# The third sum of each MLP weight set on GpSimd, from set 5 on

## The chip, the cores and the metric

The kernel runs on one core of a Trainium2 chip. The metric is the device time of one execution in microseconds (us). Each engine (TensorE or PE for matmuls, VectorE or DVE, ScalarE or ACT, GpSimd or POOL) works through its own queue in order, and so does SyncE (SP), which issues all DMAs of this kernel. Engines wait for each other through semaphores.

## The reference, cut to what matters

Two transformer blocks are applied to x, 32 sequences of 64 rows with 512 columns, all float32. The change touches only the MLP of the first block:

```python
def _L0_cond_ref(x, pos_ids, time_emb, ..., Wg, Wu, Wd):
    ...                                   # adaptive RMS norm, attention with rotary turning, x = res + ctx @ Wo.T
    res = x
    h = ada_rms(x, time_emb, ln2_w, ln2_tw)
    mlp = jax.nn.silu(h @ Wg.T) * (h @ Wu.T) @ Wd.T     # Wg, Wu: 2048 x 512, Wd: 512 x 2048
    return res + mlp
# second block: layer norm with scale and shift, latent keys and values, 16 heads of 32, x + out
```

## The kernel before, in words

The 2048 rows of x are worked in eight units of 256 rows. The MLP of a unit is cut into eight pieces (q modulo 8), each with 256 of the 2048 inner columns. A piece has three weight matrices of 2 x 2 blocks: gate (m = 0), up (m = 1) and down (m = 2). Each such product of 2 x 2 blocks is made with seven block products instead of eight, named P1 to P7, and for that each weight set needs four sums of its blocks.

A weight set is a tile `t` with seven slots of 128 x 256 float32. Slots 4 to 6 hold three blocks as they are loaded, the fourth block `a21` comes in a small tile of its own (two buffers), and slots 0 to 3 take the four sums. Slot 0 is `a21` + slot 6 (L288), slot 1 is slot 0 - slot 4 (L289), slot 2 is slot 4 - `a21` (L290), and slot 3 is slot 5 - slot 1 (L291). So the third sum (L290) needs only loaded data. The first and the third sum read `a21`, the fourth reads the second. `OF` (L254) says which product takes which slot: P1 slot 4, P6 slot 1, P5 slot 0, P7 slot 2, P2 slot 5, P3 slot 3, P4 slot 6.

The sets are numbered in the order of use: gate 0, up 0, gate 1, up 1, down 0, gate 2, up 2, down 1 and so on. The 24 sets of the first unit (numbers 0 to 22 and 25) are summed on the chip. Their four sums are written to DRAM (`done_with`, L296, "sums<-set"), and the other seven units load the finished sums from there (L274). So the sums are made once, while the MLP of the first unit runs, which in the profile is from about 60 to 155 us (sets 0 and 1 from 18 us on).

Five buffers hold the sets. When set n is done with, its sums are written out and set n + 5 is loaded (L269, and L272 for `a21`), both through SP's queue in order; a set's buffer is free when its products have been made and its write-out has read it. The load of an `a21` tile waits until the sums of the set two before it have read the old one. `combine(n + 2)` asks for the sums of a set two sets ahead of its use (L984 and L1045). Sets 0 and 1 are summed on GpSimd, the others on VectorE, but for the fourth sum, which is on GpSimd for all sets. Sets 2, 3 and 4 have their VectorE sums held behind a marked instruction (L281).

Around the sums, each piece q runs so: the first four products of gate and of up (`first_products`, L977, tile `gu` in PSUM), with ScalarE copying out P1 (L989, tile `e`) and VectorE adding P6, P5 and P7 to it (L991, L993, L996); then the first four products of the down matrix of the piece before (`down`, L1036); then the last three products of gate and up (`last_products`, VectorE's L1003), the gating (`gated`: VectorE's L1014 and GpSimd's L1015, then GpSimd's block sums L1017, L1018 and L1019 in tile `td`, which down reads), and the last three products of down. In a piece the last products of gate and up start only when L996 has read the `gu` bank.

Beside the first MLP the attention of the second unit ends, and VectorE works out the angles for units 2 and 3 (`angles(2)`, L368 to L397: many 128 x 128 operations). The order on the queues is made by the Tile framework's scheduler from the order of the program and its own model of times; the order by hand (`ordered`, `after`) holds only at the start and the end. So instructions of one engine can stand in another order than in the text.

Of the kernel before, what the change touches and what calls it, by code (L numbers as in the profile page):

```python
# [13 lines left out]
ALU = mybir.AluOpType  # L14
# [112 lines left out]
def two_blocks(ctx: ExitStack, tc: tile.TileContext, a: dict, out: bass.AP):  # L127
    nc = tc.nc
# [150 lines left out]
    def combine(n):  # L279

        with after(tc, mybir.EngineType.DVE, marks[0]) if 2 <= n < 5 else nullcontext():  # L281
            sums_of_set(n)

    def sums_of_set(n):
        if n < len(sequence) and sequence[n][1] < NP:
            t, a21 = sets[n], odd[n]
            e = nc.gpsimd if n < 2 else nc.vector
            e.tensor_tensor(t[:, 0], a21, t[:, 6], ALU.add)  # L288
            e.tensor_tensor(t[:, 1], t[:, 0], t[:, 4], ALU.subtract)  # L289
            e.tensor_tensor(t[:, 2], t[:, 4], a21, ALU.subtract)  # L290
            nc.gpsimd.tensor_tensor(t[:, 3], t[:, 5], t[:, 1], ALU.subtract)  # L291

    def done_with(m, q):
# [1006 lines left out]
```

## Time and profile before

| what | value |
|---|---|
| time of the kernel, median of 3 runs | 1027.22 us (1026.29 to 1027.46) |
| the profiled execution's own time | 1028.28 us |
| its span, first to last instruction | 1026.3 us |
| PE busy | 999.9 us (97%) |
| VectorE busy | 551.1 us (54%) |
| ScalarE busy | 327.3 us (32%) |
| GpSimd busy | 436.0 us (42%) |
| mean granted TensorE clock | 0.995 |

The execution that was profiled took 1028.28 us, 1.06 us more than the median of the runs; 1.98 us of it lie outside the span. TensorE is busy for nearly the whole span, so an operation on another engine matters only where TensorE waits for it.

### The profile page before, as it was taken

To read this page: it belongs to the slowest core of one execution; us is meant where nothing else is said; L and a number is where in the kernel's file an instruction comes from. 1 tells how busy PE (TensorE), PEld (TensorE's weight loads), DVE (VectorE), ACT (ScalarE), POOL (GpSimd) and SP (SyncE) were. 2 spreads that over 40 slices of the span, in tenths; PEclk is the share of its full clock that TensorE was granted. 3 is DMA by queue.
4 is the path that set the end of the run, shared out by engine and by line. 5 is a ranking of instruction groups with operands and counts; after the bars stand their busy time and mean duration, and the time that the engine had idled before them with its cause. 6 is when DMAs were issued, how large, how long until landed. Compare 5 with 4: busy or idle time off the path is not lost.

```text
span 1026.3 us, 21720 instructions
## 1 busy us (share of the span) xinstructions
PE 999.9 (97%) x8726; PEld 931.3 (91%) x8726; DVE 551.1 (54%) x1376; ACT 327.3 (32%) x652; POOL 436.0 (42%) x519
## 2 busy tenths in 40 slices
PE   8999899999999989999999999999999999999998
PEld 7789899988999989989989999899999899999986
DVE  5767866535355485344663366552565425554374
ACT  4432113245214242142340342242323512334032
POOL 4335546344154442346342354333553343644252
PEclk9999999999999998999999999999999999999999
DMA  9636898273555564555436755464735538751201
GB/s 349 243 120 233 274 373 302 83 252 109 194 207 181 192 242 149 200 211 204 143 117 218 258 172 191 166 230 175 288 104 195 237 119 331 290 215 38 93 1 42
DMA packets 68850, 198.54 MB, mean 193 GB/s; under 512 B 7312, under 2 KB 16272, under 8 KB 68368
## 3 DMA queue, kind: packets, MB, share of 16 engines
q1 hardware_dynamic: 68752, 197.17, 53.0%
q8 instruction: 69, 1.13, 0.4%
q14 instruction: 29, 0.24, 0.1%
HBM read 180.37 MB, written 16.78 MB: 192 GB/s over the span
## 4 chain that ended last, share of the span: by engine, by line
PE 84%; DVE 7%; DMA 3%; POOL 3%; ACT 2%; issue 1%; SPq 0%; POOLq 0%; DVEq 0%; ACTq 0%
PE gu L977 34%; PE down L1036 17%; PE q L565 11%; PE po L565 10%; DMA set<-in_wmlp 2%; PE pp L600 2%; PE sc L909 1%; PE lat L565 1%; PE kv L565 1%; PE cx L939 1%; PE sc L723 1%; PE cx L744 1%; DVE sm L593 1%; DMA stays<-in_wqkv 1%; PE tab L436 1%
## 5 line engine op out<-in xcount | busy, mean ns | idle before, releaser
L977 PE MATMUL gu<-h,set 128*128 128x128 f32 x2048 | 289.0, 278 | 7.0 <-DVE c L996 2.1
L977 PEld LDWEIGHTS gu<-h,set 128*128 128x128 f32 x2048 | 260.0, 193 | 16.3 <-issue 9.9
L977 PE MATMUL gu<-hc,set 128*128 128x128 f32 x1536 | 216.0, 277 | 0.0
L977 PEld LDWEIGHTS gu<-hc,set 128*128 128x128 f32 x1536 | 194.0, 193 | 1.6 <-issue 1.1
L1015 POOL TENSOR_TENSOR act<-c,c 128x384 f32<-128x384 f32 x64 | 66.8, 1043 | 195.8 <-DVE c L1003 158.1
L1036 PE MATMUL down<-td,set 128*128 128x128 f32 x1024 | 138.1, 277 | 2.9 <-POOL td L1018 2.1
L1036 PEld LDWEIGHTS down<-td,set 128*128 128x128 f32 x1024 | 125.5, 192 | 5.9 <-POOL td L1018 2.9
L989 ACT COPY e<-gu 128x128 f32<-128x128 f32 x128 | 33.9, 264 | 268.7 <-PE gu L977 261.8
L1003 DVE TENSOR_TENSOR c<-gu,u 128x256 f32<-128x256 f32 x128 | 53.4, 419 | 109.6 <-PE gu L977 109.1
L1036 PE MATMUL down<-act,set 128*128 128x128 f32 x768 | 109.8, 278 | 0.0
L565 PE MATMUL po<-cT,stays 128*128 128x256 f32 x480 | 108.4, 380 | 0.8 <-ACT cT L754 0.7
L565 PE MATMUL q<-h,stays 128*128 128x256 f32 x480 | 109.0, 381 | 0.0
L1036 PEld LDWEIGHTS down<-act,set 128*128 128x128 f32 x768 | 98.0, 192 | 6.0 <-issue 3.7
L991 DVE TENSOR_TENSOR u<-e,gu 128x128 f32<-128x128 f32 x128 | 36.0, 282 | 125.0 <-ACT e L989 121.3
L565 PEld LDWEIGHTS po<-cT,stays 128*128 128x128 f32 x480 | 89.3, 190 | 12.2 <-ACT cT L754 1.1
L565 PEld LDWEIGHTS q<-h,stays 128*128 128x128 f32 x480 | 89.6, 190 | 11.6 <-ACT r_a L464 0.3
L595 POOL TENSOR_TENSOR p<-p,sm 128x512 f32<-128x512 f32 x40 | 41.3, 1051 | 131.1 <-DVE sm L594 117.5
L576 POOL TENSOR_TENSOR qT<-u_q,v_q 128x512 f32<-128x512 f32 x30 | 38.1, 1271 | 88.2 <-DVE v_q L575 88.2
L621 DVE TENSOR_TENSOR x<-x,po 128x512 f32<-128x512 f32 x28 | 19.2, 685 | 72.2 <-PE po L565 70.0
L1072 ACT ACT_TABLE_LOAD x35 | 44.9, 1283 | 26.5 <-DVE c L1003 26.0
L1072 ACT ACTIVATE c<-gu 128x128 f32<-128x128 f32 x64 | 17.7, 277 | 105.2 <-DVE c L1003 104.5
L1017 POOL TENSOR_TENSOR td<-act 128x256 f32<-128x256 f32 x64 | 47.0, 734 | 5.6 <-DVE act L1014 0.9
(264 smaller groups left out, 1320.3 us busy)
## 6 DMA issues: line engine op xcount, KB each, us to landing
set<-sums SPq DMA_DIRECT2D x168, 512.0 KB, 6.6
set<-in_wmlp SPq DMA_DIRECT2D x192, 384.0 KB, 5.6
sums<-set SPq DMA_DIRECT2D x24, 512.0 KB, 4.0
x<-in_x SPq DMA_DIRECT2D x8, 512.0 KB, 5.7
mod<-in_mod SPq DMA_DIRECT2D x7, 512.0 KB, 7.9
a<-in_wmlp SPq DMA_DIRECT2D x24, 128.0 KB, 5.4
out_x<-x SPq DMA_DIRECT2D x12, 256.0 KB, 2.4
stays<-in_wo SPq DMA_DIRECT2D x2, 1024.0 KB, 9.6
```

The lines of the kernel that those rows point to most:

```text
L565: nc.tensor.matmul(ps, w[:, k, cols], h[:, k, :], start=(k == 0), stop=(k == KC - 1))
L576: nc.gpsimd.tensor_tensor(dst, u, v, ALU.add)
L595: nc.gpsimd.tensor_tensor(p8, p8, sm.unsqueeze(2).to_broadcast(wide), ALU.mult)
L600: nc.tensor.transpose(pp[:, c, :], p[:, c * P : (c + 1) * P], ident)
L977: nc.tensor.matmul(ps, w[:, slot, k * P : (k + 1) * P], b[of][:, k], start=start and k == 0, stop=k == 1, skip_group_check=True)
L989: nc.scalar.copy(e, ps[:, 0])
L991: nc.vector.tensor_tensor(u2, e, ps[:, 1], ALU.add)
L1003: nc.vector.tensor_tensor(c.rearrange("p (a b) t -> p a b t", b=2)[:, :, 1], ps[:, 2:4], u2.unsqueeze(1).to_broadcast([P, 2, HT]), ALU.add,)
L1015: nc.gpsimd.tensor_tensor(act[:, 1:4], gate[:, 1:4], c[:, 1:4], ALU.mult)
L1017: nc.gpsimd.tensor_tensor(td[:, 0:2], act[:, 1:3], act[:, 0:2], ALU.subtract)
L1036: nc.tensor.matmul(sums_of[u][p][:, c], w[:, slot, c * P : (c + 1) * P], b[of], start=q % NP == 0 and i % 2 == 0 and c == 0, stop=q % NP = ...
L1072: nc.scalar.activation(gate[2][:, 0], gate[0][:, 0], AF.Silu)
```

## The change

The third sum (slot 2) of each set from number 5 on goes to GpSimd, where VectorE made it. For sets 0 and 1 it was on GpSimd before, and for sets 2 to 4 it stays on VectorE. That makes 19 of the 24 sums of this kind (sets 5 to 22 and 25). In the kernel after the change the third sum stands at L291 and the fourth at L292; all lines from there on have a number higher by one.

```diff
             e = nc.gpsimd if n < 2 else nc.vector
             e.tensor_tensor(t[:, 0], a21, t[:, 6], ALU.add)
             e.tensor_tensor(t[:, 1], t[:, 0], t[:, 4], ALU.subtract)
-            e.tensor_tensor(t[:, 2], t[:, 4], a21, ALU.subtract)
+
+            (e if n < 5 else nc.gpsimd).tensor_tensor(t[:, 2], t[:, 4], a21, ALU.subtract)
             nc.gpsimd.tensor_tensor(t[:, 3], t[:, 5], t[:, 1], ALU.subtract)
```

## The prediction

> **What bounds the kernel now.** I read the page first, then the busy time by stage around the first MLP, the waits of TensorE there, the rows of the sums, and the order of time on VectorE and GpSimd.
>
> ```profile
> PE 999.9 (97%) x8726; PEld 931.3 (91%) x8726; DVE 551.1 (54%) x1376; ACT 327.3 (32%) x652; POOL 436.0 (42%) x519
> ```
>
> TensorE is busy for 97% of the span, so all engines together keep it waiting for 26.4 us. The change can only win where one of these waits ends on VectorE beside the first MLP. The stages there (us; then busy us and instructions of PE, weight loads, VectorE, ScalarE, GpSimd; granted clock, DMA share, GB/s):
>
> ```profile
> 60.00:98.00 38.00, 37.37 (x326) 36.07 (x327) 28.04 (x66) 10.87 (x22) 18.04 (x23) 1.00 0.64 219
> 98.00:118.00 20.00, 16.15 (x136) 15.30 (x135) 19.24 (x69) 2.57 (x9) 8.49 (x10) 1.00 0.71 236
> 118.00:152.00 34.00, 33.94 (x305) 33.77 (x303) 21.62 (x59) 4.44 (x15) 17.55 (x25) 1.00 1.01 354
> ```
>
> Only from 98 to 118 us is TensorE short of work: 20.00 - 16.15 = 3.85 us, with VectorE busy for 19.24 of 20 us (the angles are in its queue). Before it lie 0.63 us, after it 0.06 us. In the middle stage TensorE waits for (us in all, times, longest):
>
> ```profile
> PE gu L977 <- DVE ang L393: 1.5, 1, 1.5
> PE gu L977 <- DVE prod L383: 1.4, 1, 1.4
> PE gu L977 <- DVE c L996: 0.8, 2, 0.6
> PE down L1036 <- DVE set L289: 0.2, 1, 0.2
> ```
>
> All are VectorE's. The first two are named by whatever VectorE finished last; at 103.69 and 115.89 us TensorE starts last products of gate and up, which need L996, and L996 started at 103.27 and 115.47 us. So VectorE's queue ahead of L996 sets TensorE's time here. The moved sum and the ones beside it (durations: least, median, most, in ns):
>
> ```profile
> L290 DVE TENSOR_TENSOR set<-set,a x22: 410/418/1224, 62.0 to 147.7; 128x256 f32<-128x256 f32 x22
> L290 POOL TENSOR_TENSOR set<-set,a x2: 724/725/726, 18.8 to 24.2; 128x256 f32<-128x256 f32 x2
> ```
>
> The same sum takes 418 ns on VectorE and 725 ns on GpSimd. How the two engines hinder each other is seen in the order of time; these rows are from one moment (start, duration):
>
> ```profile
> 109.64 0.42 DVE L288 TENSOR_TENSOR set<-a,set 128x256 f32<-128x256 f32 x1 [0.61 <-DMA set<-in_wmlp]
> ...
> 110.45 0.28 DVE L379 TENSOR_TENSOR prod<-prod,stays 128x128 f32<-128x128 f32 x1
> 110.65 0.42 DVE L290 TENSOR_TENSOR set<-set,a 128x256 f32<-128x256 f32 x1
> 110.99 0.82 DVE L389 TENSOR_TENSOR stays<-stays,prod 128x128 f32<-128x128 f32 x1
> ```
>
> ```profile
> 110.67 0.99 POOL L291 TENSOR_TENSOR set<-set 128x256 f32<-128x256 f32 x1 [1.73 <-DVE set L289]
> ```
>
> L379 and L389 have the same kind and size; alone it takes 0.28 us, beside GpSimd's fourth sum 0.82 us, and that sum takes 0.99 us against its shortest 0.72. They exclude each other. Last, what SP's write-out of the sums waited for in the middle stage:
>
> ```profile
> SPq L296 <- DVE set L290: 7.3, 4, 2.4
> SPq L296 <- POOL set L291: 2.2, 3, 0.9
> ```
>
> **The change part by part.** The sum is made against the profiled execution: 1028.28 us, which is its span of 1026.3 and 1.98 around it. It lies 1.06 us above the median of the runs, so a difference found here is applied to the median, 1027.22 us.
>
> *Removed from VectorE:* 19 sums. The 22 rows of L290 add to 13.61 us; the three that stay (sets 2 to 4: 0.42, 0.95, 0.41) leave 11.83 us. One row starts 0.34 us after the one before it where nothing hinders it (110.65 to 110.99). Six lie in the middle stage; the last (117.14) is behind the last wait of TensorE. Five count: 5 x 0.34 = 1.7 us taken out of the queue ahead of L996. The other 13 lie where TensorE is busy throughout, but for sets 5 and 6 below: worth nothing; their cover is TensorE's own work (37.37 of 38 and 33.94 of 34 us).
>
> *Added to GpSimd:* 19 x 0.725 = 13.8 us, so its busy time goes from 436.0 to about 450 us. In the middle stage it has 20 - 8.49 = 11.5 us free, for 6 x 0.725 = 4.4. In the last stage a piece of the MLP takes 9.4 us (first down products at 122.22, 131.60 and 141.28 us); GpSimd is idle between its fourth sums there for 0.41, 0.95 and 0.95 us (from 121.34 to 126 us), which is where three sums of 0.73 fit. Queued behind a new sum are L291 of the same set, which needs L289 anyway, and at the next piece L1015 to L1019. Those have room: at 120.74 us L1018 has ended, and the product that reads it starts at 122.66. Cover gone, each sum would cost up to 0.73 us per set.
>
> *Blocking of VectorE by the new sums.* In the middle stage, ten VectorE rows of the angles are longer than the shortest of their kind and size (for the cast L368, 0.75 us, 0.28 is taken): 0.47, 0.33, 0.11, 0.65, 0.53, 0.22, 0.22, 0.54, 0.33 and 0.17, together 3.57 us, beside 8.49 us of GpSimd work. That is 0.42 us per us of GpSimd, so a sum of 0.725 us gives back 0.30 us, and five give back 1.5 us. Bounds: nothing, where VectorE is then at PSUM work or finds the gap (L991, with one input in PSUM, keeps its 0.28 us beside GpSimd), and 0.725 each, 3.6 us, where each blocks in full. I take 1.5, as it comes from the same stage and the same operations.
>
> The Trainium skill (SBUF — State Buffer, section "Who interferes with whom") says that a VectorE instruction with two SBUF inputs contends with a GpSimd instruction that reads SBUF, and that the first to issue holds the port for its whole length. The rows above agree. By that rule alone, with VectorE always at such work, each moved sum would cost 0.725 and save 0.34 us: a loss of 0.39 us each, 1.9 us for five. It is the rule that speaks against this change.
>
> *SP's queue.* No DMA is added or moved, but the write-out L296 and the next load of `a21` (L272) now wait for GpSimd's third sum. In the middle stage L296 waited 7.3 us for VectorE's L290, which stood behind angles (set 12: L288 at 104.07, L290 only at 106.88 us). On GpSimd the third sum can go as soon as the data is there. What that is worth: set 13's load was issued at 103.32 us, behind the write-out at 102.89, and VectorE sat idle 0.61 us until it landed. The write-out can't go before set 11's fourth sum (101.54 to 102.86), which comes earlier by the two L290 ahead of it, less the blocking. Bounds 0 and 0.61 us of idle time; I take 0.4 gained, nearer the upper one, since L296 is freed of its larger wait.
>
> *Sets 5 and 6.* At 78.52 us TensorE had waited 0.59 us for L621 of VectorE (77.78), which stood behind L290 rows of 0.67 and 0.96 us. Bounds: 0.59 us gained, and 0.3 lost if the new sums beside L288 and L289 block longer than what goes. I take 0.3 gained; it passes on, since set 10's load (90.69 us) waits for TensorE.
>
> Sum: -1.7 + 1.5 - 0.4 - 0.3 = -0.9 us. 1028.28 becomes 1027.4; the median 1027.22 becomes **1026.3 us**. What is late next in the middle stage is VectorE still: it keeps some 19 of 20 us. By the skill's rule in place of the measured share, the sum would be +1.9 - 0.4 - 0.3 = +1.2 us.
>
> **The rivals.** (A) *VectorE relieved in earnest.* Little blocking, as the sums fall beside PSUM work or in VectorE's idle time, and loads land earlier: the removed 1.7 us, the 0.61 and the 0.59 are won, 2.9 us, 1024.3 us. At the very most all 3.85 + 0.59 = 4.4 us of waits go: 1022.8. For it: 7.3 us of SP waits for L290. Against: the stretched rows.
>
> (B) *Slower: the new sum heads GpSimd's queue and waits for its load.* If it stands ahead of L1015, L1017 and L1018 wait for the DMA. VectorE's L288 shows when data is there: 95.98, 109.64, 120.00 and 129.85 us for the first sets of four pieces. Add 0.73 for the sum and the time from L1015's start to L1018's end (2.80, 2.53, 2.63, 2.33): `td` is ready at 99.5, 112.9, 123.4 and 132.9 us. The reading product started at 98.75, 110.68, 122.66 and 132.04. Losses 0.8 + 2.2 + 0.7 + 0.9 = 4.6; less the 0.9 gained above, +3.7 us: 1030.9. It decides once data lands over about 1.2 us after L1015 could start (in the piece at 118.11: 122.66 - 2.63 - 0.73 = 119.3). For it: the sum stands earlier in the program than L1015 and has no other input. Against: in all four pieces VectorE's L288 stands behind L1014, which starts with L1015, so the order now holds the load to come later.
>
> (C) *The order doesn't follow.* The scheduler may put VectorE's angles ahead of L996 in the freed places. Then TensorE's waits stay, and the time is that of before, 1027.2 us, with up to 1 us either way.
>
> **How the numbers follow.** My forecast, a wash to a small gain, 0.34; C 0.10; A 0.27; B 0.26; something else 0.03. A measurement of this kernel can tell about 0.2%, 2.05 us, from no change. Forecast and C lie within it for nearly all of their chance, with the forecast's ends from the bounds: -1.7 + 0 - 0.61 - 0.59 = -2.9 and -1.7 + 3.6 + 0 + 0.3 = +2.2. So: faster 0.30 (A, and the forecast's lower end), within 0.40, slower 0.30 (B, the full blocking, and part of the rest). The range takes in A and most of B: 1023.3 to 1030.6 us. The likeliest case alone: 1024.3 to 1029.4.
>
> **What would show it.** In the changed kernel the third sum is L291 and the fourth L292: 21 on GpSimd near 0.73 us and 3 on VectorE. VectorE's busy time falls by less than 11.8 us (blocking on L288, L289 and the angles). From 98 to 118 us TensorE's busy time stays at 16 to 18 us and VectorE's above 18. Waits of SP for a VectorE third sum are gone. After 160 us nothing changes. Wrong: TensorE busy there over 18.5 us (A); waits of L1036 for `td`, and GpSimd idle until a set's load in front of L1015 (B); TensorE's waits after 160 us, or the granted clock, differing by over 1 us (an order upset elsewhere).

## The result, and the profile after

The changed kernel takes 1032.65 us (median of 7 runs, 1028.43 to 1034.44); the kernel before took 1027.22 us (7 runs). The ratio is 1.0054 with a 95% interval of 1.0042 to 1.0066: the change costs about 5.4 us, and the forecast of 1026.3 us and its whole range (to 1030.6) are missed on the slow side.

The execution whose profile follows took 1034.44 us (span 1032.6 us), 1.8 us above its median. Busy time and instructions of the engines in it, from its page:

```profile
PE 999.9 (97%) x8726; PEld 930.3 (90%) x8726; DVE 550.0 (53%) x1357; ACT 327.6 (32%) x652; POOL 449.1 (43%) x538
```

The 19 instructions have moved, and GpSimd has 13.1 of the 13.8 us that were worked out for it (436.0 to 449.1). But VectorE has lost only 1.1 us of busy time (551.1 to 550.0), where instructions of 11.8 us were taken away. TensorE does the same work as before (999.9 us), in a span 6.3 us longer. The same stages beside the first MLP as in the prediction (us; then busy us and instructions of PE, weight loads, VectorE, ScalarE, GpSimd; granted clock, DMA share, GB/s):

```profile
60.00:98.00 38.00, 37.71 (x330) 36.52 (x331) 25.74 (x60) 11.12 (x22) 20.20 (x26) 1.00 0.65 221
98.00:118.00 20.00, 13.73 (x113) 12.70 (x111) 19.73 (x57) 1.49 (x5) 12.14 (x18) 1.00 0.58 196
118.00:152.00 34.00, 30.75 (x264) 29.96 (x265) 19.54 (x49) 4.72 (x16) 20.43 (x28) 1.00 0.91 308
```

TensorE is idle in the first for 0.29 us (before 0.63), in the middle one for 6.27 us (before 3.85) and in the last for 3.25 us (before 0.06). That is 5.6 us more from 98 to 152 us, about the whole loss, and a good half of it lies in the stage whose sums had been put down as covered. What TensorE waited for from 60 to 160 us (the five largest; us in all, times, longest):

```profile
PE gu L978 <- DVE c L997: 3.5, 6, 1.1
PE gu L978 <- DVE stays L379: 2.8, 2, 1.5
PE down L1037 <- POOL td L1019: 1.8, 1, 1.8
PE gu L978 <- DVE h L562: 0.8, 1, 0.8
PE down L1037 <- DVE set L289: 0.8, 1, 0.8
```

The wait for VectorE's L997 (L996 before) has grown from 0.8 to 3.5 us, and there is a new wait of 1.8 us for GpSimd's `td`, the sign that the prediction had announced for rival B. The moved sums themselves are as priced: 21 on GpSimd of 729 ns, 3 on VectorE.

```profile
L291 POOL TENSOR_TENSOR set<-set,a x21: 719/729/966, 20.1 to 155.7; 128x256 f32<-128x256 f32 x21
L291 DVE TENSOR_TENSOR set<-set,a x3: 413/418/947, 62.2 to 65.7; 128x256 f32<-128x256 f32 x3
```

**Where the new wait comes from.** GpSimd in the order of time (start, duration; in brackets the idle time before it and what ended it):

```profile
92.09 0.73 POOL L496 TENSOR_TENSOR tot_a<-sq_a 128x256 f32<-128x256 f32 x1
96.67 0.94 POOL L291 TENSOR_TENSOR set<-set,a 128x256 f32<-128x256 f32 x1 [3.86 <-DMA set<-in_wmlp]
97.58 1.17 POOL L1016 TENSOR_TENSOR act<-c,c 128x384 f32<-128x384 f32 x1
98.83 0.79 POOL L1018 TENSOR_TENSOR td<-act 128x256 f32<-128x256 f32 x1
99.69 0.52 POOL L1019 TENSOR_TENSOR td<-act,td 128x128 f32<-128x128 f32 x1
```

and the product that reads `td`:

```profile
100.26 1.60 PE L1037 MATMUL down<-td,set 128*128 128x128 f32 x12 [1.80 <-POOL td L1019]
```

The third sum of set 10 heads GpSimd's queue, and GpSimd stands idle for 3.86 us until that set's load lands. The gating (L1016), which started at 93.92 us before, starts at 97.58 us behind it, the block sums follow, and TensorE waits 1.80 us.

**Where VectorE's time went.** Its rows beside GpSimd's L1016 and L1018:

```profile
97.82 1.21 DVE L786 TENSOR_TENSOR hc<-h,hc 128x256 f32<-128x256 f32 x1
98.96 0.94 DVE L289 TENSOR_TENSOR set<-set 128x256 f32<-128x256 f32 x1
```

The same two took 0.67 and 0.41 us before. L289 makes slot 1 of set 10, which the product at 100.26 us reads too; it ended at 97.93 us before and at 99.90 us now, only 0.3 us ahead of `td`. From 60 to 160 us the means of L288 and L289 rose from 496 and 515 ns to 580 and 665 ns.

**What happened in the last stage.** SP's write-outs waited longer. From 60 to 160 us, first in the kernel before (for GpSimd and for VectorE's third sum, 69.8 us together), then in the changed one:

```profile
SPq L296 <- POOL set L291: 62.0, 15, 29.3
SPq L296 <- DVE set L290: 7.8, 5, 2.4
```

```profile
SPq L297 <- POOL set L292: 83.4, 18, 28.1
```

And they stand elsewhere. In the kernel before, SP issued the load of set 19 (L269) between the write-outs of sets 16 and 17 (L296):

```profile
122.51 0.33 SPq L296 DMA_DIRECT2D sums<-set  x1
122.89 0.42 SPq L272 DMA_DIRECT2D a<-in_wmlp  x1
123.40 1.69 SPq L269 DMA_DIRECT2D set<-in_wmlp  x2
125.20 0.38 SPq L296 DMA_DIRECT2D sums<-set  x1
```

In the changed kernel both write-outs (L297) come first, and then the loads of sets 19 to 21:

```profile
126.42 0.33 SPq L297 DMA_DIRECT2D sums<-set  x1
126.80 1.16 SPq L272 DMA_DIRECT2D a<-in_wmlp  x1
128.15 0.33 SPq L297 DMA_DIRECT2D sums<-set  x1
128.57 1.70 SPq L269 DMA_DIRECT2D set<-in_wmlp  x3
```

The write-out at 128.15 us follows at once on the end of GpSimd's fourth sum of set 17:

```profile
126.36 0.91 POOL L291 TENSOR_TENSOR set<-set,a 128x256 f32<-128x256 f32 x1
127.22 0.91 POOL L292 TENSOR_TENSOR set<-set 128x256 f32<-128x256 f32 x1
```

Counted from the first down product of set 16 (122.22 us before, 125.12 after), the load of set 19 is issued 3.45 us later where it was 1.18. VectorE's first sum of that set starts 10.30 us after the same product, where it was 7.63 (at 129.85 us):

```profile
135.42 0.42 DVE L288 TENSOR_TENSOR set<-a,set 128x256 f32<-128x256 f32 x1 [4.12 <-issue]
```

No DMA had been edited. The scheduler, which orders every queue by its own model of times, had moved the write-outs of sets 12, 17 and 20 in front of the loads of sets 14 and 15, of 19 and 20, and of 22.

### The profile page after: what moved, and what is told of

Same layout as the page of the kernel before. It is cut to its first block, busy times and chain, and to the rows that moved or that the text cites. A ratio compares the mean times of both kernels' runs of the same rounds, so it can differ in the third digit from the quotient of the medians.

```text
span 1032.6 us, 21704 instructions
## 1 busy us (share of the span) xinstructions
PE 999.9 (97%) x8726; PEld 930.3 (90%) x8726; DVE 550.0 (53%) x1357; ACT 327.6 (32%) x652; POOL 449.1 (43%) x538
## 3 DMA queue, kind: packets, MB, share of 16 engines
q8 instruction: 70, 1.15, 0.4%
## 4 chain that ended last, share of the span: by engine, by line
PE 84%; DVE 7%; POOL 3%; DMA 2%; issue 1%; ACT 1%; SPq 0%; POOLq 0%; DVEq 0%; ACTq 0%
PE gu L978 34%; PE down L1037 17%; PE q L566 11%; PE po L566 10%; PE pp L601 2%; PE sc L910 1%; PE lat L566 1%; PE kv L566 1%; PE cx L940 1%; DMA set<-in_wmlp 1%; PE sc L724 1%; PE cx L745 1%; DVE sm L594 1%; PE tab L437 1%; DMA mod<-in_mod 1%
## 5 line engine op out<-in xcount | busy, mean ns | idle before, releaser
L1016 POOL TENSOR_TENSOR act<-c,c 128x384 f32<-128x384 f32 x64 | 66.7, 1042 | 197.7 <-DVE c L1004 154.8
L566 PEld LDWEIGHTS q<-h,stays 128*128 128x128 f32 x480 | 89.5, 190 | 11.8 <-ACT r_a L465 0.3
L1018 POOL TENSOR_TENSOR td<-act 128x256 f32<-128x256 f32 x64 | 47.1, 736 | 5.4 <-DVE act L1015 0.6
```

The lines of the kernel that those rows point to most:

```text
L566: nc.tensor.matmul(ps, w[:, k, cols], h[:, k, :], start=(k == 0), stop=(k == KC - 1))
L1016: nc.gpsimd.tensor_tensor(act[:, 1:4], gate[:, 1:4], c[:, 1:4], ALU.mult)
L1018: nc.gpsimd.tensor_tensor(td[:, 0:2], act[:, 1:3], act[:, 0:2], ALU.subtract)
```

## The experiments

Three theories were set against each other. **Queue (Q):** the sum of set 10 at the head of GpSimd's queue makes `td` late. **SP's order (S):** loads are issued behind write-outs that wait for GpSimd. **Blocking (X):** GpSimd's sums hold up VectorE by more than is taken from it. Ratios are to the kernel before on the same chip in the same session (medians 1026.50, 1026.82 and 1027.01 us), with 95% intervals. A table of all kernels' stages stands at the end.

In the recorded expectations X is called P; O stands for a new order on VectorE and SP, and L for write-outs and loads that are late because GpSimd's fourth sums are.

The mean clock granted in an execution differs (0.991 to 1.000), and the time follows it. So some differences are also given *at equal clock*: one straight line of time against clock through the 204 executions of all kernels whose clock is on record, with a level of its own for each kernel and session, has a slope of 0.83 us per 0.001 of clock, and the levels are compared (with 95% limits). This is an estimate from those runs.

### The two halves of the change apart

*The relief alone.* From set 5 on, ScalarE copies a block into slot 2 and no engine makes the third sum; the subtraction is left out.

```diff
-            (e if n < 5 else nc.gpsimd).tensor_tensor(t[:, 2], t[:, 4], a21, ALU.subtract)
+            if n < 5:
+                e.tensor_tensor(t[:, 2], t[:, 4], a21, ALU.subtract)
+            else:
+                nc.scalar.copy(t[:, 2], t[:, 4])
```

> From set 5 on the third sum is left out and ScalarE copies its first operand (slot 4) to slot 2 instead: the subtraction is missing, so the numbers are not the reference's. VectorE is relieved as in the changed kernel and has its order (but for two neighbours swapped), SP has exactly its order; GpSimd's work and order are those of the kernel before. Theory P or Q (the loss is GpSimd's): the loss goes, 1027.2 us or less, down to 1024.3 if VectorE's relief is won in full. Theory O (order of VectorE and SP): 1030 us or more.

Measured: 1025.37 us, 0.9984 [0.9975, 0.9993], 1.1 us below the kernel before by the medians, 1.6 by the ratio and 0.8 +- 0.7 at equal clock. VectorE is busy for 544.0 us, 7.1 less.

*The load alone.* The kernel before, in which GpSimd makes each third sum from set 5 on once more into a tile that nobody reads. The order on the other four queues is that of before.

```diff
             e.tensor_tensor(t[:, 2], t[:, 4], a21, ALU.subtract)
+            if n >= 5:
+                junk = work("junk", [P, 2 * P], f"junk_{n}", 1)
+                nc.gpsimd.tensor_tensor(junk, t[:, 4], a21, ALU.subtract)
```

> The kernel before with 19 sums more: from set 5 on GpSimd makes the third sum once more into a tile that nobody reads, and VectorE keeps its own. PE, VectorE, ScalarE and SP have exactly the order of the kernel before; GpSimd has nearly that of the changed kernel, the extra sum of set 10 ahead of L1016 too. Theory P or Q (GpSimd's added work alone does it): as slow as the changed kernel or slower, 1032 us or more, as VectorE isn't relieved here. Theory O: 1029.5 us or less.

Measured: 1032.5 us, 1.0058 [1.0043, 1.0072], 6.0 us slower, with 1.01 us of waiting for `td` and 0.40 us for VectorE's third sum (L291 in this kernel). Engines' busy time, first the relief alone, then the load alone:

```profile
PE 996.9 (97%) x8726; PEld 928.6 (91%) x8726; DVE 544.0 (53%) x1357; ACT 334.3 (33%) x671; POOL 434.5 (42%) x519
```

```profile
PE 1001.1 (97%) x8726; PEld 931.7 (90%) x8726; DVE 558.6 (54%) x1376; ACT 327.2 (32%) x652; POOL 450.8 (44%) x538
```

VectorE's work in the second is that of before, yet it is busy for 7.5 us more: 0.39 us for each of the 19 sums. The changed kernel against the first gives (550.0 - 544.0) / 19 = 0.32 us. The other kernels with 19 moved sums give less: 0.28 with SP's order held, 0.22 with set 10's sum held, and 0.21 with both (549.3, 548.2 and 547.9 us). The prediction had 0.30, for the middle stage. So blocking is there, over the whole kernel at about the forecast's size; for the middle stage by itself no run gives it. And not all that VectorE gets back comes from the new sums: with none of them it has lost 7.1 us where rows of 11.8 us were taken away. The load costs several times what the relief brings, and nearly all of it in the middle stage (29.09 us from set 10 to set 16 against 23.91); the last stage runs at TensorE's full pace (28.14 us).

### The queue

*The sum of set 10 behind `td`.* The third sum of set 10 is held until GpSimd has issued the last block sum of `td` of that piece; the order on the other queues stays.

```diff
-            (e if n < 5 else nc.gpsimd).tensor_tensor(t[:, 2], t[:, 4], a21, ALU.subtract)
+            with after(tc, mybir.EngineType.Pool, ends_td[2]) if n == 10 else nullcontext():
+                (e if n < 5 else nc.gpsimd).tensor_tensor(t[:, 2], t[:, 4], a21, ALU.subtract)
...
+        ends_td[q] = latest(tc, mybir.EngineType.Pool)      # end of td, in gated
```

> The changed kernel with one difference: on GpSimd the third sum of set 10 is held behind the block sums of td of the piece before (L1020 of piece 2); all other instructions stand in the same order on all engines. Theory Q (the loss is GpSimd's queue waiting for set 10's load, 3.86 us in front of L1016, for which TensorE then waits 1.80 us): the wait of TensorE for td at 100.3 us goes, and the time falls from 1032.65 by 1.8 us or more, to 1030.9 or, if the later waits are its consequence, to about 1028. Theory P (the shared port: GpSimd's added work holds VectorE up): the time stays within 1 us of 1032.65. Theory O (the new order on VectorE and SP): it stays within 1 us too.

Measured: 1029.84 us, 1.0039 [1.0024, 1.0055]. The wait for `td` is gone; 0.60 us of waiting for VectorE's L289 stands at its place:

```profile
99.42 1.57 PE L1039 MATMUL down<-td,set 128*128 128x128 f32 x12 [0.60 <-DVE set L289]
```

*The sum of set 10 left on VectorE.*

```diff
-            (e if n < 5 else nc.gpsimd).tensor_tensor(t[:, 2], t[:, 4], a21, ALU.subtract)
+            (nc.gpsimd if n < 2 or (n >= 5 and n != 10) else e).tensor_tensor(t[:, 2], t[:, 4], a21, ALU.subtract)
```

> The changed kernel with the third sum of set 10 alone back on VectorE (18 moved sums are left). Theory Q: GpSimd no longer waits for that load in front of L1016, TensorE's 1.80 us wait for td goes: 1030.9 us or less. Theory P: one sum of 19 less on GpSimd, a gain of 0.3 us at most. Theory O: depends on the order that results; the order on VectorE after the angles is another one here, so a change either way of up to 2 us.

Measured: 1027.86 us, 1.0018 [1.0004, 1.0032]. Here 1.38 us of waiting for L289 stand in place of the 1.80 us for `td`. One of 19 sums left where it was takes away two thirds of the loss, but not by that wait alone: set 10's load landed only at 98.1 us in the profiled execution, and the load of set 19, too, is issued 2.82 us after the first down product of set 16, where the changed kernel has 3.45.

### Which sets cost

Only sets 5 to 9, only 10 to 15, or all from 16 on go to GpSimd:

```diff
-            (e if n < 5 else nc.gpsimd).tensor_tensor(t[:, 2], t[:, 4], a21, ALU.subtract)
+            (nc.gpsimd if 5 <= n < 10 else e).tensor_tensor(t[:, 2], t[:, 4], a21, ALU.subtract)
```

In the others the bounds are 10 and 16, and 16 and 26; `e` stays GpSimd for sets 0 and 1 and VectorE for the rest.

> Only the third sums of sets 5 to 9 on GpSimd, the others on VectorE; PE and SP have the order of the kernel before. The prediction's step on sets 5 and 6: a gain of up to 0.59 us (TensorE's wait for L621 at 78.5 us goes), about 1026.2 us, if nothing is blocked; a port effect here would show as a loss of at most 0.5 us, as TensorE is busy from 79 to 100 us.

> Only the third sums of sets 10 to 15 on GpSimd, in the stage where VectorE has no room. If the loss comes from this stage (queue in front of L1016 and blocking among the angles): +4 us or more, 1030.5 us and up. If the later sets make their own loss: +2 to +3.5 us.

> Only the third sums of sets 16 to 22 and 25 on GpSimd, in the stage where TensorE was busy for 33.94 of 34 us. The prediction's step (worth nothing there, as GpSimd's idle time of 2.3 us a piece holds the three sums): within 0.5 us of before, 1026 to 1027 us. If the changed kernel's waits between 127 and 142 us (2.4 us) are made by these sets themselves: +2 us or more.

Measured: sets 5 to 9, 1026.88 us, 1.0001 [0.9987, 1.0015]; sets 10 to 15, 1032.35 us, 1.0046 [1.0030, 1.0061]; from set 16 on, 1026.76 us, 0.9997 [0.9987, 1.0008]. The six sums of the stage where VectorE has no room cost nearly all of it, with the wait for `td` (1.18 us). Those from set 16 on cost nothing by themselves; in that kernel the last stage reads:

```profile
118.00:152.00 34.00, 34.00 (x307) 34.00 (x306) 19.96 (x52) 4.57 (x15) 23.41 (x32) 1.00 1.00 352
```

TensorE is never idle, though GpSimd is busy for 23.41 us, more than in the changed kernel (20.43). So it isn't GpSimd's load in the last stage that cost 3.25 us there in the changed kernel. That stage was entered with loads already late, or has another order.

### SP's order

*The order of before on SP.* In the changed kernel, SP's loads and write-outs of sets 10 to 22 are chained in the order of the kernel before, with no wait between them.

```diff
+    SP_ORDER = 'L10 L11 L12 a12 W10 a13 W11 L13 L14 a14 L15 W12 a15 W13 a16 W14 L16 L17 a17 L18 a18 W15 a19 W16 a20 L19 L20 W17 L21 a21 W18 a22 W19 L22 W20'.split()
...
+    for one, other in zip(SP_ORDER, SP_ORDER[1:]):
+        tc.add_manual_dep(issue[other], issue[one].name, info, reason="order")
```

(L is the load of a set, a that of its `a21`, W its write-out.)

> The changed kernel with SP's loads and write-outs of sets 10 to 22 held in the order of the kernel before (the loads of sets 13, 14, 19, 20 and 22 again ahead of the write-outs of 12, 17 and 20); GpSimd's order is that of the changed kernel. I look at the time from the first product of the first MLP to the first down product of set 25: 90.62 us before, 96.69 changed. Theory S (from set 16 on the loss is made on SP: write-outs that wait for GpSimd's late fourth sums stand in front of loads): the 3.4 us lost between the first down products of sets 16 and 25 shrink to under 1 us; time of the stage about 93.5, of the kernel about 1029.5 us. If it is made by blocking or by GpSimd's load itself: the stage stays at 96 us or more, the kernel at 1032.

Measured: 1029.37 us, 1.0029 [1.0016, 1.0041]. The wait for `td` stays (1.29 us). SP in the last stage (its write-outs are L300, its loads L270 and L274 here):

```profile
125.15 0.33 SPq L300 DMA_DIRECT2D sums<-set  x1
125.53 0.42 SPq L274 DMA_DIRECT2D a<-in_wmlp  x1
126.05 1.90 SPq L270 DMA_DIRECT2D set<-in_wmlp  x2
128.04 0.38 SPq L300 DMA_DIRECT2D sums<-set  x1
```

The write-out of set 17 comes no earlier than in the changed kernel, against TensorE, but the loads of sets 19 and 20 no longer stand behind it: 1.15 us after the first down product of set 16 (124.90 us). The stretch from the first product to the first down product of set 25 is 93.29 us, about what theory S had said (93.5). The expectation names the loads of sets 13 and 14; in the rows it is those of 14 and 15 that stood behind the write-out of set 12.

*Both holds*, on set 10's sum and on SP's order:

> Both holds at once: SP's order of the kernel before, and set 10's third sum on GpSimd behind td of piece 2. If Q, S and the blocking add up, what is left is the blocking less the relief in the middle stage: stage time 91.5 to 92.5 us, kernel 1027 to 1029 us.

Measured: 1028.12 us, 1.0009 [0.9998, 1.0020]. By the ratio the loss is no longer told from zero; at equal clock 1.5 +- 0.6 us are left. In the profiled execution set 10's load came late, and 1.70 us of waiting for its second sum (L292 here) stand where the other kernel waited 1.29 us for `td`: in these two traces Q's gain isn't seen, only in the medians (1029.37 and 1028.12). The stretch to set 25 is 93.22 us, longer than the 91.5 to 92.5 that were expected.

The two holds make a square of four kernels. As differences of the ratios times 1027 us: Q: 1.5 us (1.0054 to 1.0039) and 2.1 us (1.0029 to 1.0009). S: 2.6 us (1.0054 to 1.0029) and 3.1 us (1.0039 to 1.0009). Each single difference has an uncertainty of about 1.7 to 2.0 us (the half intervals added in squares), the mean of each pair about 1.3: Q 1.8, S 2.8, together 4.6 of 5.5 us. At equal clock S is 3.2 +- 0.9 and 2.2 +- 0.9 us, Q 1.4 +- 1.0 and 0.4 +- 0.8: the kernel with SP's order held alone had the lower clock (0.9962 on average, against 0.9977 with both holds). So S is shown in both pairs; Q is shown only while SP has the new order, and there barely.

### Fills in place of sums

The kernel with set 10's sum held, in which GpSimd fills slot 2 twice with a constant where it made the third sum, held in the same order. The third sum is left out. A fill takes 0.31 us and the two 0.68 us together, so GpSimd is nearly as busy; but it reads nothing, and waits for no load.

```diff
-                (e if n < 5 else nc.gpsimd).tensor_tensor(t[:, 2], t[:, 4], a21, ALU.subtract)
...
+                mark = ends_td[(n - 4) // 3] if n % 3 == 1 else third[n - 1] if n == 11 else fourth[10] if n == 12 else fourth[n - 1]
+                with after(tc, mybir.EngineType.Pool, mark):
+                    nc.gpsimd.memset(t[:, 2], 0.01)
+                    nc.gpsimd.memset(t[:, 2], 0.01)
...
```

> Like the run with set 10's sum behind td, but from set 5 on GpSimd fills slot 2 with a constant, twice (two fills of 128x256 should take about 0.62 us, between the measured 0.20 for 128x128 and 0.52 for 128x512 each, against 0.73 for the sum), where it made the third sum: the sum is left out, so the numbers are not the reference's. PE, VectorE, ScalarE and SP have exactly the order of that run. GpSimd is occupied for nearly as long, but reads nothing. Theory P (GpSimd's reading sum and VectorE's operations with two SBUF inputs shut each other out): most of that run's loss of 3.3 us goes, 1027.5 us or less. Theory L (GpSimd is simply later with the fourth sums, so write-outs and the loads behind them on SP are later): 1029 us or more remains.

Measured: 1028.33 us, 1.0009 [0.9998, 1.0020], against 1.0039 [1.0024, 1.0055] with the sums. VectorE is busy for 544.4 us, as with no third sum at all (544.0), where it is 548.2 with the sums in the same order. L289 takes 504 ns on average, where it takes 654 with those sums (L288 takes 538 and 543): the fills hardly block VectorE, the sums do. The time lies between the two forecasts. The difference of 0.0030 +- 0.0019 (3.0 +- 0.9 us at equal clock) isn't all blocking, though, since the fills don't wait for a load either. This run doesn't part the two: VectorE's time is blocking, but the time of the kernel can be either.

### The angles out of the way

If VectorE has room in the middle stage, does the change gain? `angles` is made at the sixth piece instead, in the kernel before and in the changed one.

```diff
+            if q == 5:
+                later_angles()
...
-    ahead = Job(attention0(1, {"ring": "1", "lean": True}, late=later_angles), A0)
+    ahead = Job(attention0(1, {"ring": "1", "lean": True}, late=None), A0)
```

> The kernel before with the angles for units 2 and 3 asked for at piece 5 of the first MLP and no longer at the end of the second unit's attention; nothing else is edited, sums as before. If VectorE's queue in the middle stage is what TensorE waits for, its 3.85 us there go, for the most part: stage time 87 to 88 us and 3 us less in all, 1023.5 us; unless the angles make new waits at the later pieces (then 1026 us or more).

> The changed kernel with the angles at piece 5 as well. If the change's loss in the middle stage needs the angles (blocking of their two-input operations): stage 118 to 98 us as good as in the run with late angles alone, and the change costs under 2.5 us against that run (set 10's queue of 1.8 us and SP's order stay). If GpSimd's added work costs by itself: 4 us or more against that run.

Measured: before with late angles 1027.06 us, 1.0002 [0.9988, 1.0015]; changed with late angles 1034.95 us, 1.0077 [1.0061, 1.0093]. In the first the middle stage becomes 2.6 us shorter (21.32 us from set 10 to set 16, against 23.91) and the next one 5.0 us longer (33.42 against 28.44): the waits go with the angles, and nothing is gained. Between the two runs the change costs 0.0075, or 7.7 us, and at equal clock 5.2 +- 1.0 us, about as much as with the angles in their old place; `td` is waited for longer (1.96 us). So the loss doesn't hang on the angles standing just there.

### All kernels by stage

From the first gate product of the first MLP (60.04 us in the kernel before) to the first down product of set 10, on to that of set 16, and on to that of set 25, read off TensorE's rows in the order of time; one profiled execution each. At TensorE's pace a piece is 9.38 us, so the last stage is 28.14 us at best. The last column is the time from the first down product of set 16 to the issue of set 19's load.

| kernel | to 10 | 10 to 16 | 16 to 25 | load of 19 issued |
|---|---|---|---|---|
| before | 38.27 | 23.91 | 28.44 | 1.18 |
| sums of sets 16 to 25 alone | 38.27 | 23.20 | 28.14 | 1.23 |
| sums of sets 5 to 9 alone | 37.57 | 23.75 | 28.14 | 1.00 |
| load alone (sums twice) | 38.86 | 29.09 | 28.14 | 1.21 |
| SP's order and set 10 held | 37.56 | 26.91 | 28.75 | 1.14 |
| SP's order held | 37.56 | 26.97 | 28.76 | 1.15 |
| relief alone | 37.57 | 22.84 | 29.25 | 2.57 |
| set 10 on VectorE | 37.91 | 27.07 | 29.16 | 2.82 |
| sets 10 to 15 alone | 38.82 | 26.67 | 30.04 | 2.83 |
| fills, set 10 held | 37.57 | 23.50 | 30.71 | 3.48 |
| changed, set 10 held | 38.07 | 25.59 | 31.50 | 3.52 |
| changed | 37.56 | 27.27 | 31.86 | 3.45 |
| before, late angles | 38.16 | 21.32 | 33.42 | 6.07 |
| changed, late angles | 37.56 | 26.13 | 34.46 | 6.66 |

The length of the last stage goes with the issue of that load: 28.1 to 28.8 us where it is issued after 1.0 to 1.2 us, 29.2 to 30.0 at 2.6 to 2.8, 30.7 to 31.9 at 3.5 (in the last two rows the angles stand in that stage as well). Where SP keeps the order of before, the last stage is nearly whole, however much GpSimd has to do (the sums of sets 16 to 25 alone, the load alone, and the two kernels with SP's order held). The new order by itself costs little: the kernel with the relief alone has exactly the changed kernel's order on SP, its last stage is 0.8 us longer than before, and it is the fastest of all. It becomes dear when GpSimd is late, as the write-outs in front of the loads wait for it.

In the middle stage the kernels with GpSimd's sums of sets 10 to 15 (or 11 to 15) take 25.6 to 29.1 us and those without 22.8 to 23.9 (with the angles in their old place). Two kernels that do the same up to set 16, before and the sums of sets 16 to 25 alone, differ by 0.7 us there, so small differences inside the first group are not read. With both holds the middle stage is still 3.0 us longer than before, the last 0.3 longer and the first 0.7 shorter.

## Why the prediction was wrong

**Right.** The sums' durations (725 ns taken, 729 measured), their number on each engine, GpSimd's total (450 forecast, 449.1), the blocking of a sum (0.30 taken, 0.21 to 0.39 measured as a mean over the whole kernel), the 0.59 us wait of sets 5 and 6, which is gone (the stretch to set 10 is 0.71 us shorter), and that nothing changes after 160 us: past the first MLP the same work follows in the same order, and where the two traces drift apart by up to 1.4 us, the granted clock differs. That relief and blocking would nearly cancel is neither shown nor refuted: with both holds 0.9 us of loss are left by the ratio [-0.2, 2.1], 1.5 +- 0.6 us at equal clock, where the sum without SP's term said -0.5 with bounds of -2.3 and +2.2. It lies within the bounds, but more likely on the slow side. That TensorE would be busy for 16 to 18 us from 98 to 118 us failed: it was 13.73.

The Trainium skill (SBUF — State Buffer, "Who interferes with whom") holds that the first instruction on the shared port keeps the other out for its whole length. Measured over all 19 sums the blocking is 0.21 to 0.39 us of 0.73 on average, so the full length at every sum was too dear here, though the rule pointed the right way. The same section says that a VectorE instruction with two SBUF inputs doesn't contend with a GpSimd instruction that only writes; the run with fills agrees (L289 at 504 ns, 515 in the kernel before, and 654 with GpSimd's sums in the same order).

**The step "SP's queue": -0.4 us, measured +2.8 (3.2 and 2.2 at equal clock).** This is the step that failed by most, and its sign was wrong. It took the order of SP's queue as given and asked only which wait each write-out loses. But the order is the scheduler's, and it changed when the sums left VectorE: the kernel with the relief alone, where nothing is added on GpSimd, has the new order, and the one with the load alone, where VectorE keeps its sums, has that of before. The write-outs of sets 12, 17 and 20 went ahead of loads, and wait for GpSimd's fourth sums, which now stand behind third sums. The bounds "0 and 0.61" held no loss, since no row of before showed one; a reordered queue had no term.

**The step "Queued behind a new sum... Those have room": wrong at set 10, where TensorE waited 1.80 us.** The room at L1015 to L1019 was read off one piece (120.74 to 122.66 us) and said of all. Rival B had the right mechanism and was priced at four pieces: 0.8 + 2.2 + 0.7 + 0.9 us. It came true at the first alone, where the wait is 1.80 us instead of 0.8, as the data came later (the sum starts at 96.67 us, not at 95.98: 0.7 us), the sum itself took 0.94 us, not 0.73 (0.2), and TensorE was ready for the product at 98.46 us, not at 98.75 (0.3); the rest, from L1016's start on, went 0.2 us quicker than priced. But the wait isn't the price. Had `td` been in time, that product would still have waited for L289 to 99.90 us, 1.4 of the 1.8 us, unless L289 too had come earlier: set 10's data came later (0.6 us), and L785, L786 and L289 together took 1.3 us longer beside GpSimd's new sum and the gating behind it. The hold of that sum brought 1.8 +- 1.3 us by the ratios, 1.4 and 0.4 at equal clock. The prediction treated queue and blocking as separate terms; here they meet at one product. B's reason was not the right one, either: the program asks for set 10's sums after the gating of that piece, and the scheduler put the sum first all the same. At sets 13, 16 and 19 it put the gating first.

**The step "the other 13 sums are worth nothing, their cover is TensorE's own work".** True of the sums from set 16 on by themselves, and of 5 to 9. Not true once SP's loads come late: from 118 to 152 us TensorE was short of work for 3.25 us (0.06 before).

**The rivals.** A (relief in earnest) is refuted for the change: VectorE gained 1.1 us of its busy time. Its 2.9 us are not reached even with nothing put on GpSimd: 1.1 us by the medians, 1.6 by the ratio. Of B, the first of its four pieces came true. C (the order doesn't follow) was nearest to S, but looked at VectorE's queue only, and had the time unchanged.

**What stays open.** How the remaining loss (0.9 us by the ratio, 1.5 at equal clock) divides into blocking and late sums, and how much of the wait at set 10 is the queue's and how much the blocking's; and whether the fills are cheap because they read nothing or because they wait for nothing. No kernel here is measurably better than the one before and still computes all of it: the sums of sets 5 to 9 alone, or of 16 to 25 alone, make no difference that can be told.

## What to carry to other kernels

An instruction that moves to another engine is to be priced by the queue that it enters: whether its input arrives later than the inputs of what stands behind it, at every place and not at one. Where a scheduler writes the queues, compare the order of all of them, the DMA issuer's too, since moving a sum off one engine reordered here what nobody had edited; a write-out in front of a load cost little here until the engine that it waits for was late. And where two engines hinder each other, what is taken from the one can come back as stretched instructions: of 11.8 us of VectorE's rows removed, 7.1 us of busy time were gained with no new work on GpSimd, and 1.1 us with the sums there.

## What was not expected of the hardware

A GpSimd fill of 128x256 float32 took 0.31 us and left VectorE's second sum (L289) at 504 ns on average, where a GpSimd sum of that size took 0.73 us and, in the same order, stretched it to 654 ns. The mean granted clock of one execution lay between 0.991 and 1.000, and times follow it by some microseconds: the kernel before took 1024.3 and 1025.5 us at 1.000 and 1028.3 to 1029.7 us at 0.995; the changed one 1028.4 and 1028.6 us at 1.000 and 1032.2 to 1034.4 us at 0.995 to 0.997. The loss shows at each clock.
